# An adaLN attention and mixture-of-experts kernel: sorted tiles transposed by their loads and VectorE, the last three tiles' results brought by products on chip, key and value products four steps later

## The chip, the cores and the metric

The kernel runs on one core of a Trainium2 chip. A core has a TensorE for matrix products, VectorE, ScalarE and GpSimd for the rest, SyncE for issuing transfers, and 16 DMA engines. The metric is the time of one execution on the device in microseconds, as a median over runs. One further execution is taken by the hardware profiler, and the views of the profile and trace come from it.

## What is computed

All data are 32-bit floats. The input is 2 batches of 1024 tokens of 256 numbers. First comes attention, with 16 heads of 128 and one key and value head, on a normalised and modulated input; then a mixture of experts: each token goes to its two best of eight experts.

```python
h = layernorm(x) * (1 + ca) + sa
x = x + ga * attention(h, ...)
h = layernorm(x) * (1 + cb) + sb
logits = h @ router_w.T
topk_vals, topk_idx = top_k(logits, 2); topk_w = softmax(topk_vals)
# rows sorted by expert, then for each expert's rows:
y1 = x_sorted @ w1[e].T                # 256 -> 2 x 176
y2 = (silu(y1[:, :176]) * y1[:, 176:]) @ w2[e].T    # 176 -> 256
y = sum over the two experts of y2 * topk_w
x = x + gb * y
```

## The kernel before

**Attention.** Tokens are cut into 16 tiles of 128. Queries are worked on in four blocks of 512 tokens; in each block a loop runs over 16 heads and 8 key tiles, 128 steps (h, j), each with a product of queries and keys (line 767), an exponential on ScalarE (771) and a product with the values (782). Other work is hung on named steps by `at(h, j, f)`: among it, in the first two blocks, what batch 1's tokens need: normalisation, transposition of the input through DRAM, key and value products (`prep_kv`) and a transposition of the keys (`prep_turned`), at lines 1509 to 1515. In the last block the first twelve token tiles' rows are placed and scattered to DRAM, sorted by expert (`sorted_x`), and the experts' weights are loaded (`load_w1`, line 350). `clear_sorted` (337) fills `sorted_x` with zeros beforehand, in the third block.

**The experts.** The sorted rows make 39 tiles of 128 rows (`ALL`), since each expert's part is rounded up; a row carries 256 numbers and a tail of four: its weight, its place among the results, its batch. Tiles 0 to 16 (`FULL`) hold rows of the first twelve token tiles alone and can be loaded early. Tiles 17 to 38 need the rows of the last four token tiles too, and those are placed and scattered while the first tiles are worked on (`place_second`, eight scatters on GpSimd, hung on the loop at m = 8 and 9). A tile goes through these methods of class `Sorted`:

- `__init__`: one SyncE transfer of 128 rows of 1040 B (1587), issued seven tiles ahead.
- `turn`: two TensorE transposes "xp" (1594) and a ScalarE copy to "xT" (1596), since the product needs the 256 numbers along the partitions.
- `up`: two products "su" of two passes each with the first weight matrix (1603), SiLU on ScalarE "sg" (1611), multiplication on VectorE "sact" (1613).
- `turn_back`: two TensorE transposes "ap" (1619) and a ScalarE copy "sactT" (1621).
- `down`: two products "sy" of two passes each with the second matrix (1628), VectorE's "ysb" (1636), which reads PSUM and multiplies by weight and gate, and an indirect scatter on GpSimd to `results` in DRAM (1639).
- `gates`: VectorE blends the two batches' output gates for tiles 0 to 31 (1656).

The loop at line 1699 emits `turn` of tile m, `up` of m-1, `turn_back` of m-3 and `down` of m-4 (from m = 24 on, one less each). When tile 31's results are scattered, the first twelve token tiles' results can be fetched (`fetch`, 1664, 256 KB a token tile: two rows a token), and `combine` adds the two rows and the residual `xs` on VectorE (1676, 1677) and sends the sum out (1678). The tail (1731 to 1753) adds some of these beside the last tiles, then waits for the last scatter and fetches and adds the last four token tiles.

**What sets the order.** The program names what each engine does, and a planner of the framework puts the instructions of each engine into one order, by modelled costs and the time at which something is due; `tc.issue_after` pins an instruction behind another. Each engine then works through its queue in this order. Transfers from SyncE and ScalarE go over eight lanes in turn, and each waits for the one eight before it. A vector transpose (`turned`, 432, uses it elsewhere) turns each 32 x 32 block of a tile in place of the whole tile.

Of the kernel before, what the change touches and what calls it, by code (L numbers as in the profile page):

```python
# [60 lines left out]
def tile_adaln_attention_moe(  # L61
# [38 lines left out]
    ONES = TOP * SETS[0][1] + E  # L100
    ALL = (TOP * NT * P + E * (P - 1)) // P
    PARTS = 3

    xt = x.rearrange("b (t p) d -> p (b t) d", p=P)
    ot = out.rearrange("b (t p) d -> p (b t) d", p=P)
# [141 lines left out]
    with ExitStack() as attn:  # L247
# [88 lines left out]

        def clear_sorted():

            zero = work.tile([P, ROW], FP, tag="h", name="zero")
            nc.vector.memset(zero, 0.0)  # L340
            by_tile = sorted_x.rearrange("(m p) d -> p m d", p=P)
            nc.sync.dma_start(out=by_tile, in_=zero.unsqueeze(1).to_broadcast([P, ALL, ROW]))
            nobody = work.tile([P, ALL, 1], I32, tag="z", name="nobody")
            nc.gpsimd.iota(nobody, [[P, ALL]], base=TOP * NT * P, channel_multiplier=1)
            with nc.allow_non_contiguous_dma(reason="one number of each row"):
                nc.sync.dma_start(out=by_tile[:, :, TO : TO + 1].bitcast(I32), in_=nobody)
# [1 line left out]
        w1_at = []  # L348

        def load_w1():  # L350
            w1_in = w1.rearrange("(c p) e i -> p c e i", p=P)
            pieces = []
            for c in range(DC):
                piece = keep.tile([P, E, I2], FP, tag="w1" + "ab"[c], name=f"w1_{c}")
                nc.sync.dma_start(out=piece, in_=w1_in[:, c])
                pieces.append(piece)
            w1_at.append(pieces)

# [1075 lines left out]
        for blk in range(NBLK):  # L1434
# [7 lines left out]
            def at(h, j, f, *a):  # L1442
                besides[h * NJ + j].append(lambda: f(*a))
# [62 lines left out]
                    at(QT + 3 + n, 3, on_vector, scatter_some, k, t, 3)  # L1506
                at(HEADS - HG + 1, 0, load_w2)

            for i, h in enumerate(((6, 8, 11, 13), (7, 9, 11, 13))[blk] if blk < 2 else ()):
                t = TPB + blk * QT + i  # L1510
                if t < NT:
                    at(h, 1, prep_norm, t)
                    at(h, 3, prep_input, t)
                    at(h + 1, 5, prep_kv, t)
                    at(h + 1, 7, prep_turned, t)
            last = attention(blk, q, steps, besides)
            settle = Settle(blk)
            if after is None:
# [15 lines left out]
    with ExitStack() as moe:  # L1534
# [28 lines left out]
        def expert(m):  # L1563
# [10 lines left out]
                loaded.update(zip(range(m, m1), values))  # L1574
            return loaded[m]

        class Sorted:


            def __init__(self, m):  # L1580
                self.m = m
                if m < EARLY + NEXT:
                    pool = mx if m < EARLY else me
                    self.x = pool.tile([P, ROW], FP, name=f"x_{m}")
                else:
                    self.x = row_buffer(f"x_{m}")[:, :ROW]
                load = nc.sync.dma_start(out=self.x, in_=sorted_x[ts(m, P), :])
                into_x.read(load, TOP * (SETS[0][1] if m < FULL else NT))

            def turn(self):  # L1590
                m = self.m
                tp = ps_t.tile([P, DC, P], FP, tag="t", name=f"xp_{m}")
                for c in range(DC):
                    nc.tensor.transpose(tp[:, c, :], self.x[:, ts(c, P)], ident)  # L1594
                self.xT = mg.tile([P, DC, P], FP, tag="xT", name=f"xT_{m}")
                nc.scalar.copy(self.xT, tp)  # L1596

            def up(self):
                m = self.m
# [15 lines left out]
            def turn_back(self):  # L1615
                m = self.m
                tp = ps_t.tile([P, 2, P], FP, tag="t", name=f"ap_{m}")
                for c in range(2):
                    nc.tensor.transpose(tp[:, c, :], self.act[:, ts(c, P)], ident)  # L1619
                self.actT = mg.tile([P, 2, P], FP, tag="sactT", name=f"sactT_{m}")  # L1620
                nc.scalar.copy(self.actT, tp)

            def down(self):
                m = self.m
                at = expert(m) * (2 * D)
                y = ps_y.tile([P, D], FP, tag="y", name=f"sy_{m}")
                for c in range(2):
                    nc.tensor.matmul(  # L1628
                        y,
                        self.actT[:, c, :],  # L1630
                        w2_flat[:, c * D :][:, bass.ds(at, D)],
                        start=(c == 0),
                        stop=(c == 1),
                    )
                ysb = mg.tile([P, D], FP, tag="ysb", name=f"ysb_{m}", bufs=5)
                self.evicted = nc.vector.scalar_tensor_tensor(  # L1636
                    ysb, y, self.x[:, WEIGHT : WEIGHT + 1], self.gate, ALU.mult, ALU.mult
                )
                ins = nc.gpsimd.indirect_dma_start(  # L1639
                    out=results,  # L1640
                    out_offset=bass.IndirectOffsetOnAxis(
                        ap=self.x[:, TO : TO + 1].bitcast(I32), axis=0
                    ),
                    in_=ysb,
                    in_offset=None,
                )
                self.scattered = ins.ins
                into_results.add(ins)

            def gates(self):  # L1650

# [9 lines left out]
        def fetch(t, queue=nc.sync):  # L1661

            y = row_buffer(f"y_{t}").rearrange("p (k d) -> p k d", k=TOP)
            load = queue.dma_start(
                out=y,
                in_=results[TOP * t * P : TOP * (t + 1) * P, :].rearrange(
                    "(p k) d -> p k d", k=TOP
                ),
            )
            into_results.read(load, ONES if t < SETS[0][1] else ALL)  # L1670
            return y

        def combine(t, y, queue):

            sum_ = y[:, 0, :]
            nc.vector.tensor_tensor(sum_, sum_, y[:, 1, :], ALU.add)
            nc.vector.tensor_tensor(sum_, sum_, xs[:, t, :], ALU.add)
            queue.dma_start(out=ot[:, t, :], in_=sum_)

        settle.pools(mg, ms, ps_t, "t")  # L1680
        gb_more = mg.tile([P, D], FP, name="gb_more", bufs=1)
        nc.vector.tensor_tensor(gb_more, gb[:, 1, :], gb[:, 0, :], ALU.subtract)
        tiles = []
        fetched, have = [], 0
        back = done = 0
# [9 lines left out]
            7: [lambda: count(NBLK - 1, mg, ps_t, "t"), lambda: place_second(mg, settle.shares)],  # L1695
        }
        SCATTERS = 8
        LATER = 24
        for m in range(ALL + 3):
            there = ALL if m >= SCATTERS + TOP else FULL  # L1700
            while len(tiles) < min(m + 1 + PRE, there):
                tiles.append(Sorted(len(tiles)))
            for f in late.get(m, ()):
                f()
            if m < ALL:
                tiles[m].turn()
            if 0 <= m - 1 < ALL:
                tiles[m - 1].up()
            sooner = m >= LATER
            while back < min(m - 2 + sooner, ALL):  # L1710
                tiles[back].gates()
                tiles[back].turn_back()
                back += 1
            while done < min(m - 3 + sooner, ALL):
                tiles[done].down()
                done += 1
            if SCATTERS <= m < SCATTERS + TOP:
                k = m - SCATTERS
                with tc.issue_after(tiles[done - 1].scattered):
                    if k:  # L1720
                        choose_second(*SETS[1])
                    for t in range(*SETS[1]):
                        scatter(place_i[:, t, k : k + 1], t)

            for t in range(have, min(max(have, 2 * (done - ONES)), SETS[0][1])):
                fetched.append((t, fetch(t)))
                have = t + 1
        assert have == SETS[0][1] and done == ALL


        def added(some, behind, queue):
            with tc.issue_after(behind):
                for t, y in some:
                    combine(t, y, queue)

        BESIDE = 5
        for i in range(BESIDE):
            m = ALL - 4 + i // 2
            added(
                fetched[i : i + 1],  # L1740
                tiles[m].evicted.ins if i % 2 else tiles[m + 1].active.ins,
                nc.sync,
            )
        sent = mg.tile([P, 1], FP, name="sent", bufs=1)
        with tc.issue_after(tiles[-1].scattered):
            nc.gpsimd.memset(sent, 0.0)
        seen = mg.tile([P, 1], FP, name="seen", bufs=1)
        with tc.issue_after(tiles[-1].evicted.ins):
            look = nc.vector.tensor_copy(seen, sent).ins
        lasts = [(t, fetch(t, (nc.sync, nc.scalar)[t % 2])) for t in range(*SETS[1])]  # L1750
        added(fetched[BESIDE:], look, nc.scalar)
        for t, y in lasts:
            combine(t, y, (nc.sync, nc.scalar)[t % 2])


_OUT = ((2, 1024, 256), "float32")
# [41 lines left out]
```

## Time and profile before

| | us |
|---|---|
| median of 3 runs | 1266.76 (1266.58 to 1268.63) |
| the profiled execution | 1273.54 |
| its span | 1271.8 |
| TensorE busy, whole span | 1244.7 (98%) |
| VectorE busy | 848.5 (67%) |
| ScalarE busy | 452.7 (36%) |
| GpSimd busy | 187.3 (15%) |
| expert stage, from about | 1148 |

The span runs from the first to the last record of the profiled execution. Engine names in the profile: PE is TensorE, PEld its weight loads, DVE is VectorE, ACT is ScalarE, POOL is GpSimd, SPq is SyncE's transfer issue. In a row of groups, `out<-in xcount | busy, mean ns | idle before, releaser`, the last field is the idle time of the engine just before these instructions and what ended most of it. In the chain of waits a row is start, length and what ran; in the timeline it is start, length, engine, line, instruction, shape and count, with the idle time before it in brackets. Matmul starts are recorded and their ends modelled, so the pitch of consecutive starts tells more of TensorE's pace than a duration does.

### The profile page before, as it was taken

What the parts mean: (1) busy time and instruction counts of PE and PEld (TensorE: products, weight loads), DVE (VectorE), ACT (ScalarE), POOL (GpSimd) and SP (SyncE); (2) the same over time, 40 slices, a digit from 0 to 9 for tenths busy, and PEclk for the clock granted to TensorE, in tenths of its full rate; (3) what the DMA queues carried; (4) which work ended last, traced back from release to release, by engine and by line L of the source; (5) the groups of instructions that cost most, each with busy time, mean ns of one, the idle gap of its engine ahead of it and who ended that gap; (6) DMA issues with size and microseconds to landing.
All of it is one profiled execution on the core that took longest, in us unless ns stands there. A gap on an engine that the chain in (4) does not pass through costs nothing.

```text
span 1271.8 us, 13505 instructions
## 1 busy us (share of the span) xinstructions
PE 1244.7 (98%) x4134; PEld 686.0 (54%) x4134; DVE 848.5 (67%) x1763; ACT 452.7 (36%) x884; POOL 187.3 (15%) x223
## 2 busy tenths in 40 slices
PE   8999999999999999999999999999999999999895
PEld 5544444448545454548545454557545444477573
DVE  7577777666866876666866666666758675547355
ACT  3533333331333343431333434321333344314331
POOL 3210301010100201010000000000000223204542
PEclk9999999999999999999999999999999999999998
DMA  7011020211011111111011061012011242113426
GB/s 265 0 34 34 6 83 15 73 35 42 13 44 44 40 48 43 49 38 35 12 51 38 34 198 34 34 54 76 13 56 32 68 141 92 34 34 97 134 84 236
DMA packets 87975, 79.26 MB, mean 62 GB/s; under 512 B 43520, under 2 KB 66688, under 8 KB 87648
## 3 DMA queue, kind: packets, MB, share of 16 engines
q1 hardware_dynamic: 82624, 67.06, 17.3%
q0 software_dynamic: 3408, 9.38, 2.0%
q10 hardware_dynamic: 1872, 1.97, 0.4%
q8 instruction: 34, 0.56, 0.2%
q14 instruction: 37, 0.30, 0.1%
HBM read 58.29 MB, written 20.08 MB: 62 GB/s over the span
## 4 chain that ended last, share of the span: by engine, by line
PE 90%; DVE 3%; POOL 2%; issue 2%; DMA 1%; another core or an unknown queue 0%; ACT 0%; SPq 0%; POOLq 0%; DVEq 0%; ACTq 0%
PE s L767 34%; PE o L782 33%; PE q L693 7%; PE pr L925 6%; PE pr L846 2%; PE su L1603 2%; PE sy L1628 1%; POOL results L1639 1%; PE kv L466 1%; PE q L642 1%; PE ap L1619 0%; PE xp L1594 0%; PE lg L1051 0%; DMA wide_q<-row_q 0%; DVE h L404 0%
## 5 line engine op out<-in xcount | busy, mean ns | idle before, releaser
L767 PE MATMUL s<-qT,kT 128*128 128x512 f32 x1024 | 524.4, 595 | 0.7 <-ACT qT L1310 0.7
L782 PE MATMUL o<-p,vs 128*128 128x512 f32 x1024 | 521.6, 592 | 0.0
L771 ACT ACTIVATE p<-s 128x512 f32<-128x512 f32 x512 | 304.8, 597 | 511.3 <-PE s L767 498.1
L787 DVE TENSOR_TENSOR sum<-sum,p 128x512 f32<-128x512 f32 x384 | 264.2, 688 | 178.8 <-ACT p L771 175.9
L782 PEld LDWEIGHTS o<-p,vs 128*128 128x128 f32 x1024 | 194.3, 190 | 243.5 <-issue 238.7
L767 PEld LDWEIGHTS s<-qT,kT 128*128 128x128 f32 x1024 | 191.5, 190 | 186.4 <-issue 177.2
L742 POOL TENSOR_TENSOR rn_q<-rn_q,minus_half 128x16 f32<-128x16 f32 x15 | 44.1, 2940 | 319.0 <-DVE rn_q L738 300.4
L787 DVE TENSOR_TENSOR sum<-p,p 128x512 f32<-128x512 f32 x64 | 43.9, 685 | 38.5 <-ACT p L771 38.5
L1603 PE MATMUL su<-w,xT 128*128 x156 | 54.2, 471 | 3.6 <-ACT xT L1596 3.5
L551 DVE STREAM_TRANSPOSE turned_q<-sq_q 128x512 f32<-128x512 f32 x60 | 42.4, 707 | 18.2 <-ACT sq_q L655 18.2
L925 PE MATMUL pr<-wout_sb,qT 128*128 128x128 f32 x384 | 50.0, 276 | 0.0
L583 DVE TENSOR_TENSOR qT<-qT,wide_q 128x512 f32<-128x512 f32 x60 | 41.1, 686 | 10.7 <-DMA wide_q<-row_q 10.7
L583 DVE TENSOR_TENSOR qT<-qT,wide 128x512 f32<-128x512 f32 x64 | 43.5, 679 | 6.9 <-DMA wide<-row 6.8
L1639 POOL DMA_INDIRECT results<-ysb,x x39 | 40.4, 1037 | 50.5 <-DVE ysb L1636 39.2
L655 ACT ACTIVATE sq_q<-qT 128x512 f32<-128x512 f32 x56 | 35.2, 629 | 34.6 <-DVE qT L700 26.9
L551 DVE STREAM_TRANSPOSE turned<-sum 128x512 f32<-128x512 f32 x64 | 45.5, 710 | 1.8
L925 PEld LDWEIGHTS pr<-wout_sb,qT 128*128 128x128 f32 x384 | 46.2, 192 | 0.1
L693 PE MATMUL q<-rows,wq_sb 128*128 128x256 f32 x168 | 45.4, 379 | 0.0
L789 ACT COPY qT<-o 128x512 f32<-128x512 f32 x64 | 37.4, 584 | 19.7 <-PE o L782 19.6
L552 DVE TENSOR_REDUCE parts<-turned 128x16 f32<-128x512 f32 x64 | 43.3, 676 | 1.1
L1628 PE MATMUL sy<-w2s,sactT 128*128 x156 | 40.3, 383 | 1.5 <-issue 1.3
L552 DVE TENSOR_REDUCE parts_q<-turned_q 128x16 f32<-128x512 f32 x60 | 40.8, 680 | 0.7
(330 smaller groups left out, 1067.9 us busy)
## 6 DMA issues: line engine op xcount, KB each, us to landing
wide<-row SPq DMA_DIRECT2D x64, 256.0 KB
wide_q<-row_q SPq DMA_DIRECT2D x60, 256.0 KB
sorted_x<-zero SPq DMA_DIRECT2D x1, 5070.0 KB
x<-sorted_x SPq DMA_DIRECT2D x39, 130.0 KB
y<-results SPq DMA_DIRECT2D x14, 256.0 KB
w<-in_w_dram SPq DMA_DIRECT2D x2, 1408.0 KB
wout_sb<-in_wout_dram SPq DMA_DIRECT2D x1, 2048.0 KB
wq_sb<-in_wq_dram SPq DMA_DIRECT2D x1, 1536.0 KB
```

The costliest lines, as they stand in the source:

```text
L551: nc.vector.transpose(turned.rearrange("p c k -> p (c k)"), src)
L552: latest["vector"] = nc.vector.tensor_reduce(parts[:, i, :], turned, AX.X, ALU.add).ins
L583: nc.vector.tensor_tensor(q.head(h), q.head(h), wide, ALU.mult)
L693: nc.tensor.matmul(ps[:, k, :].rearrange("p (t k) -> p t k", k=P), x, y, start=True, stop=True,)
L767: latest["tensor"] = nc.tensor.matmul(s, kT[:, ts(b * NJ + j, P)], q.head(h), start=True, stop=True).ins
L771: nc.scalar.activation(p, s, AF.Exp)
L782: latest["tensor"] = nc.tensor.matmul(outs[h], vs[:, b * NJ + j, :], p, start=(j == 0), stop=(j == NJ - 1)).ins
L787: latest["vector"] = nc.vector.tensor_tensor(sums[h], first, p, ALU.add).ins
L925: nc.tensor.matmul(ps[:, piece, :], halves(g)[:, pair, head, t, i, :], w[:, g * HG // TWO + pair, :], start=False, stop=(g == NG - 1 and m ...
L1603: nc.tensor.matmul(u, self.xT[:, c, :], w1_flat[c][:, bass.ds(at, I2)], start=(c == 0), stop=(c == DC - 1),)
L1628: nc.tensor.matmul(y, self.actT[:, c, :], w2_flat[:, c * D :][:, bass.ds(at, D)], start=(c == 0), stop=(c == 1),)
L1639: ins = nc.gpsimd.indirect_dma_start(out=results, out_offset=bass.IndirectOffsetOnAxis(ap=self.x[:, TO : TO + 1].bitcast(I32), axis=0), in ...
```

## The change

- Tiles of sorted rows: for tiles 0 to 7, three transfers each replace one (the tail, and two halves of the 256 numbers written in permuted column order); the TensorE transposes stay. For tiles 8 to 38 five transfers each replace one: the tail of 16 B a row, and four which each fill 32 partitions with 4 x 64 numbers from four rows; then VectorE's transpose of 32 x 32 blocks writes "xT" in one instruction. The rows of the first weight matrix are permuted to match, so that it is loaded by eight transfers in place of two.
- The last three tiles (`HERE`) are no longer scattered. For each, `find` builds a one-hot matrix (128 x 512) of which of the last 512 tokens a row belongs to, and twelve products on TensorE add the three tiles' results into PSUM tiles "direct", which VectorE adds to `xs`. The last four token tiles are therefore fetched after the scatter of tile 35; their rows of `results` are zeroed by `clear_sorted`, since not every row is then written.
- In the first two blocks, `prep_kv` and `prep_turned` are hung four steps later, and the last of the four tiles one head sooner.

```diff
+    HERE = 3
 ...
             nc.sync.dma_start(out=by_tile, in_=zero.unsqueeze(1).to_broadcast([P, ALL, ROW]))
+            lo, hi = [TOP * t * P for t in SETS[1]]
+            nc.sync.dma_start(
+                out=results[lo:hi, :].rearrange("(m p) d -> p m d", p=P),
+                in_=zero[:, :D].unsqueeze(1).to_broadcast([P, (hi - lo) // P, D]),
+            )
...
-            w1_in = w1.rearrange("(c p) e i -> p c e i", p=P)
+            w1_in = w1.rearrange("(b c j) e i -> c b j e i", c=DC, j=SIDE)
...
-                nc.sync.dma_start(out=piece, in_=w1_in[:, c])
+                for b in range(P // SIDE):
+                    nc.sync.dma_start(out=piece[ts(b, SIDE)], in_=w1_in[c, b])
...
-            for i, h in enumerate(((6, 8, 11, 13), (7, 9, 11, 13))[blk] if blk < 2 else ()):
+            for i, h in enumerate(((6, 8, 11, 12), (7, 9, 11, 12))[blk] if blk < 2 else ()):
...
-                    at(h + 1, 5, prep_kv, t)
-                    at(h + 1, 7, prep_turned, t)
+                    at(h + 2, 1, prep_kv, t)
+                    at(h + 2, 3, prep_turned, t)
...
+        FIRST_TILES = 8
+        in_blocks = sorted_x.rearrange("(m a i) d -> m i a d", a=P // SIDE, i=SIDE)
...
-                load = nc.sync.dma_start(out=self.x, in_=sorted_x[ts(m, P), :])
-                into_x.read(load, TOP * (SETS[0][1] if m < FULL else NT))
+                n = D // (P // SIDE)
+                parts = [(self.x[:, D:], sorted_x[ts(m, P), D:])]
+                if m < FIRST_TILES:
+                    src = sorted_x[ts(m, P), :D].rearrange("p (b c j) -> c p b j", c=DC, j=SIDE)
+                    for c in range(DC):
+                        parts.append((self.x[:, ts(c, P)].rearrange("p (b j) -> p b j", j=SIDE), src[c]))
+                else:
+                    for b in range(P // SIDE):
+                        to = self.x[ts(b, SIDE), :D].rearrange("i (a k) -> i a k", k=n)
+                        parts.append((to, in_blocks[m][:, :, ts(b, n)]))
+                for to, src in parts:
+                    with nc.allow_non_contiguous_dma(reason="some numbers of each row"):
+                        load = nc.sync.dma_start(out=to, in_=src)
+                    into_x.read(load, TOP * (SETS[0][1] if m < FULL else NT))
 
             def turn(self):
...
+                nc.vector.transpose(
+                    self.xT.rearrange("p c (a i) -> p a c i", i=SIDE),
+                    self.x[:, :D].rearrange("p (a c j) -> p a c j", c=DC, j=SIDE),
+                )
...
+                if m >= ALL - HERE:
+                    return
                 ins = nc.gpsimd.indirect_dma_start(
...
+            def find(self):
+                half = mg.tile([P, 1], I32, tag="half", name=f"half_{self.m}")
+                nc.vector.tensor_scalar(
+                    half, self.x[:, TO : TO + 1].bitcast(I32), 1, None, ALU.arith_shift_right
+                )
+                token = mg.tile([P, 1], FP, tag="token", name=f"token_{self.m}")
+                nc.vector.tensor_copy(token, half)
+                self.at = mg.tile([P, QB], FP, name=f"at_{self.m}", bufs=1)
+                nc.vector.tensor_scalar(self.at, tokens, token, None, ALU.is_equal)
...
-            into_results.read(load, ONES if t < SETS[0][1] else ALL)
+            into_results.read(load, ONES if t < SETS[0][1] else ALL - HERE)
...
+            if m == TOKENS:
+                nc.gpsimd.iota(token_i, [[1, QB]], base=SETS[1][0] * P, channel_multiplier=0)
+                nc.vector.tensor_copy(tokens, token_i)
+            if FIND <= m - 4 < FIND + HERE:
+                tiles[m - 4 - FIND + ALL - HERE].find()
...
-        lasts = [(t, fetch(t, (nc.sync, nc.scalar)[t % 2])) for t in range(*SETS[1])]
...
+        lasts = [(t, fetch(t)) for t in range(*SETS[1])]
...
+            for tile_ in some:
+                nc.tensor.matmul(
+                    direct[t],
+                    tile_.at[:, ts(i, P)],
+                    tile_.ysb,
+                    start=(tile_ is here[0]),
+                    stop=(tile_ is here[-1]),
+                )
...
+        with tc.issue_after(last_at):
+            for t in range(t0, t1):
+                nc.vector.tensor_tensor(xs[:, t, :], direct[t], xs[:, t, :], ALU.add)
+            for t, y in lasts:
+                combine(t, y, (nc.sync, nc.scalar)[t % 2])
```

More of the change, by code (lines that the diff above doesn't have):

```diff
@@ L102, in tile_adaln_attention_moe @@
     PARTS = 3
+    HERE = 3
+    assert ALL - HERE >= ONES
     xt = x.rearrange("b (t p) d -> p (b t) d", p=P)
@@ L1586, in __init__ @@
                     self.x = row_buffer(f"x_{m}")[:, :ROW]
-                load = nc.sync.dma_start(out=self.x, in_=sorted_x[ts(m, P), :])
-                into_x.read(load, TOP * (SETS[0][1] if m < FULL else NT))
-            def turn(self):
[L1591 to L1596, printed above, removed]
+                n = D // (P // SIDE)
[12 more added lines that the diff above has]
+                    into_x.read(load, TOP * (SETS[0][1] if m < FULL else NT))
+            def turn(self):
+                self.xT = mg.tile([P, DC, P], FP, tag="xT", name=f"xT_{self.m}")
+                if self.m < FIRST_TILES:
+                    tp = ps_t.tile([P, DC, P], FP, tag="t", name=f"xp_{self.m}")
+                    for c in range(DC):
+                        nc.tensor.transpose(tp[:, c, :], self.x[:, ts(c, P)], ident)
+                    nc.scalar.copy(self.xT, tp)
+                    return
[3 more added lines that the diff above has]
+                )
             def up(self):
@@ L1620, in turn_back @@
                 self.actT = mg.tile([P, 2, P], FP, tag="sactT", name=f"sactT_{m}")
-                nc.scalar.copy(self.actT, tp)
+                self.copied = nc.scalar.copy(self.actT, tp).ins
             def down(self):
@@ L1635, in down @@
                 ysb = mg.tile([P, D], FP, tag="ysb", name=f"ysb_{m}", bufs=5)
+                self.ysb = ysb
                 self.evicted = nc.vector.scalar_tensor_tensor(
@@ L1638, in down @@
                 )
+                if m >= ALL - HERE:
+                    return
                 ins = nc.gpsimd.indirect_dma_start(
@@ L1676, in combine @@
             nc.vector.tensor_tensor(sum_, sum_, y[:, 1, :], ALU.add)
-            nc.vector.tensor_tensor(sum_, sum_, xs[:, t, :], ALU.add)
-            queue.dma_start(out=ot[:, t, :], in_=sum_)
+            last = nc.vector.tensor_tensor(sum_, sum_, xs[:, t, :], ALU.add).ins
+            if queue is nc.scalar:
+                with tc.issue_after(tiles[-1].copied):
+                    queue.dma_start(out=ot[:, t, :], in_=sum_)
+            else:
+                queue.dma_start(out=ot[:, t, :], in_=sum_)
+            return last
         settle.pools(mg, ms, ps_t, "t")
@@ L1682, in tile_adaln_attention_moe @@
         nc.vector.tensor_tensor(gb_more, gb[:, 1, :], gb[:, 0, :], ALU.subtract)
+        token_i = mg.tile([P, QB], I32, name="token_i", bufs=1)
+        tokens = mg.tile([P, QB], FP, name="tokens", bufs=1)
         tiles = []
@@ L1697, in tile_adaln_attention_moe @@
         SCATTERS = 8
+        TOKENS, FIND = 20, 27
         LATER = 24
@@ L1728, in tile_adaln_attention_moe @@
         assert have == SETS[0][1] and done == ALL
[L1731 to L1749, printed above, removed]
-        lasts = [(t, fetch(t, (nc.sync, nc.scalar)[t % 2])) for t in range(*SETS[1])]
-        added(fetched[BESIDE:], look, nc.scalar)
-        for t, y in lasts:
-            combine(t, y, (nc.sync, nc.scalar)[t % 2])
+        lasts = [(t, fetch(t)) for t in range(*SETS[1])]
@@ new lines, in tile_adaln_attention_moe, with bring @@
+        direct = {}
+        def bring(t, some):
+            i = t - SETS[1][0]
+            if t not in direct:
+                pool, tag = ((ps_u, "u"), (ps_t, "t"))[i // TWO]
+                direct[t] = pool.tile([P, D], FP, tag=tag, name=f"direct_{t}")
+            for tile_ in some:
[6 more added lines that the diff above has]
+                )
@@ new lines, in tile_adaln_attention_moe @@
+        here = tiles[ALL - HERE :]
+        t0, t1 = SETS[1]
+        for some in (here[:-1], here[-1:]):
+            for t in range(t0, t0 + TWO):
+                bring(t, some)
+        for t in range(t0 + TWO, t1):
+            bring(t, here)
+        behind = [tiles[ALL - 4 + i // 2 + 1 - i % 2] for i in range(5)]
+        behind = [a.evicted.ins if i % 2 else a.active.ins for i, a in enumerate(behind)]
+        behind += [tiles[ALL - 2].evicted.ins]
+        last_at = None
+        for i, (t, y) in enumerate(fetched):
+            with tc.issue_after(behind[i] if i < len(behind) else last_at or tiles[-1].evicted.ins):
+                last_at = combine(t, y, nc.scalar if i >= len(behind) else nc.sync)
```

## The prediction

> **What bounds the kernel now.** I read the engine totals first, then TensorE's costliest groups.
>
> ```profile
> PE 1244.7 (98%) x4134; PEld 686.0 (54%) x4134; DVE 848.5 (67%) x1763; ACT 452.7 (36%) x884; POOL 187.3 (15%) x223
> ...
> L1603 PE MATMUL su<-w,xT 128*128 x156 | 54.2, 471 | 3.6 <-ACT xT L1596 3.5
> ...
> L1628 PE MATMUL sy<-w2s,sactT 128*128 x156 | 40.3, 383 | 1.5 <-issue 1.3
> ```
>
> TensorE is busy for 98% of the span; nothing that only relieves another engine can pay. The expert stage (from 1148 us) is the last tenth of the span. The chain of waits there is TensorE alone:
>
> ```profile
> 1211.42 1.19 PE su L1603 x4
> 1212.61 0.22 PE ap L1619 x2
> 1212.83 0.86 PE sy L1628 x4
> 1213.69 0.22 PE xp L1594 x2
> 1213.91 1.19 PE su L1603 x4
> ```
>
> One tile costs 1.19 + 0.22 + 0.86 + 0.22 = 2.49 us of TensorE with no gap. The reason is the order on its queue: between su_m and ap_m stand the products of other tiles (ap_{m-1}, sy_{m-2}, xp_{m+2} and su_{m+1} in the late part), so SiLU, multiply and copy of tile m run under them. What one tile takes when nothing stands between is read from the timeline, and from the one place where TensorE did wait for the copy:
>
> ```profile
> 1244.69 1.35 PE L1603 MATMUL su<-w,xT 128*128 x4
> ...
> 1246.08 0.32 ACT L1611 ACTIVATE sg<-su 128x176 f32<-128x176 f32 x1 [0.76 <-PE su L1603]
> ...
> 1246.43 0.34 DVE L1613 TENSOR_TENSOR sact<-sg,su 128x176 f32<-128x176 f32 x1 [1.27 <-ACT sg L1611]
> ```
>
> ```profile
> 1180.01 0.37 ACT L1621 COPY sactT<-ap 128x256 f32<-128x256 f32 x1
> ...
> 1180.43 0.92 PE L1628 MATMUL sy<-w2s,sactT 128*128 x3 [0.16 <-ACT sactT L1621]
> ```
>
> After the last pass of su the SiLU starts 1.39 us behind su's start, the multiply 0.35 later; the copy of ap starts 0.47 us behind ap (1245.88 to 1246.35), and sy 0.42 behind that copy.
>
> Last, the waits of TensorE:
>
> ```profile
> PE su L1603 <- ACT xT L1596: 3.5, 2, 2.8
> ...
> PE kv L466 <- DMA rows<-turned_z: 1.2, 1, 1.2
> ```
>
> The 2.8 us belong to a stall over tiles 11 to 15: su_11 to su_15 take 17.63 us instead of 4 x 2.49, so 7.67 too many, with the granted clock at 0.5 for 3.4 us at its end. The profiled execution took 1273.54 us, 6.8 over the median of 1266.76, about this stall. I take it for an event of that execution and work in its times less 7.67 us: su_38 at 1251.94 - 7.67 = 1244.3, end of span 1264.1 = su_38 + 19.86; the median lies 2.7 above.
>
> **The change, part by part.**
>
> *Block loads and vector transposes, the gain intended.* Two TensorE transposes go for 31 tiles: 31 x 0.22 = 6.8 us of the bound engine. The ScalarE copy (0.37) goes, VectorE gets one transpose per tile:
>
> ```profile
> 141.27 0.43 DVE L437 STREAM_TRANSPOSE blocks_z<-z 128x256 f32<-128x256 f32 x1
> ...
> 1148.08 2.22 SPq L1587 DMA_DIRECT2D x<-sorted_x  x5
> ```
>
> VectorE per tile: 0.48 + 0.48 + 0.34 + 0.43 = 1.73 us of 2.49, not a bound by itself. SyncE issues five loads in place of one, 2.22 / 4.67 pitches = 0.475 us each: 2.375 per tile (five of 130 KB in that row go out at this pitch; small ones, the key rows, do as well).
>
> *The order on the queues, where I put the cost.* The instruction order of the changed kernel as built is not the old one less xp. Tiles 8 to 13 keep it; 14 to 16 use up the lead; for tiles 17 to 20 TensorE has su_m, sy_{m-1}, ap_m, su_{m+1}; from tile 21 it has su_m, ap_m, sy_m, su_{m+1}, ap_{m+1}, sy_{m+1}, to the end. On VectorE the transpose of tile m+1 stands behind the multiply of tile m. TensorE takes its queue in order, so nothing covers ScalarE and VectorE any more. One period, from su's start: multiply at 1.39 + 0.35 = 1.74; it takes 0.34 and TensorE follows 0.05 later (the gap in front of the sy row above): ap at 2.13; copy at +0.47 = 2.60; sy at +0.42 = 3.02; sy's passes 0.87: su_{m+1} at **3.9 us**. xT_{m+1} (done 2.08 + 0.43) is ready by then. Against 2.49, each tile loses 1.41, 0.22 saved included. For tiles 17 to 20 the evicting multiply of sy_{m-1} stands before xT_{m+1} on VectorE: su 1.19, sy 0.87 to 2.06, about 0.2 to the eviction, 0.48, gate and transpose 0.43 to 0.9: 3.27 per tile; the step into 21 about 3.46.
>
> *Where the slow part starts.* Tile 17 needs the second set of scattered rows. Copying the token numbers (128x512) adds about 0.55 to VectorE's chain at the stage's start; the transposes of tiles 8 to 10 add 3 x 0.43 = 1.3 in VectorE's solid stretch (1163 to 1175) ahead of the placing; one more result scatter ahead of the set's last four on GpSimd adds its pitch, 1.27. SyncE's first load of x_17, 1186.2 before, is then at some 1188.8; the fifth follows 1.9 later and lands about 2.4 on (single loads took 1.9 to 2.5): 1193.1, plus the transpose and lost lead: su_17 at about 1194.5 (1191.15 before). su_21: 1194.5 + 3 x 3.27 + 3.46 = 1207.8. su_38: 1207.8 + 17 x 3.9 = 1274.1, against 1244.3: **+29.8 us**.
>
> *The last three tiles.* The old end after su_38: the last scatter, 3.59 us to land, and a 2.99 us fetch before the last additions. The new end waits for VectorE: ysb_38 at about su_38 + 5.4, fourteen additions at 0.38 = 5.3, four of the products at 0.42 = 1.7, eight at 0.38 = 3.0, and 3.7 from the last addition to the end as before: 19.1. The twelve products (two passes each, 12 x 0.43 = 5.2 us by a 256-column pass's 0.217) run under these additions but for two that stand ahead of sy_38, 0.9, within the 5.4 counted. Gain 0.8; if VectorE's additions take the 0.42 of single ones, -0.1. The fetches of the last four token tiles start after tile 35's scatter, over 5 us before they are needed at this pace. The finding (three vector operations, at most 0.9 us by a 128x512 row of 0.7) lies in VectorE's slack of 3.9 - 1.73.
>
> *Keys and values four steps later.* They can remove the 1.2 us wait at 165.23, no more: -1.2, between 0 and -1.2. Their products keep their length.
>
> *At nothing:* the eight weight loads in place of two (SyncE has no transfer due there, 352 KB pieces, landed 80 us before use; uncovered they would cost 6 x 0.475), and 1 MB more of cleared rows, about 3 us behind a 15 us write, with SyncE's next transfer 13 us after its end.
>
> *Two rules of the Trainium skill.* First, "DMA: Bandwidth & Descriptors", Rules for kernel authors: coalesce many small transfers, transfers to parts of the partitions use the same engines and gain nothing. The change does the reverse. By the row, issue pitch is 0.475 and the path is not SyncE's while tiles take 3.9: nothing. By the rule (under 64 KB one pays mostly overhead) the five 32 KB pieces would cost up to five of the 1.9 us latencies in sequence, 9.5 per tile; eight are in flight at once, and the key rows of this kernel go out and land eight deep, so I stay with the row. Second, "TensorE: Matmul & The Clock Gate", Why this matters for your kernels: no idle gap over some 3 us, else half clock; its Part 1 adds that frequent short idles between groups can also make the clock swing. Here 2.82 us idle was followed by 0.5, while idle shares of 19 to 24% (1180 to 1184) and of 60 to 65% (1184 to 1188) still showed 1.00. The new gaps are 0.9 and 0.7 us, 42% of each period. By the first rule nothing happens; by the second the passes double: 3.9 + 2.27 = 6.2 per tile, +40 us more. The nearest rows are the gaps of 0.69 and 1.31 us, at full clock; I take no loss and keep the other for the range.
>
> Sum: +29.8 - 0.8 - 1.2 = +27.8; span 1264.1 + 27.8 = 1291.9, plus 2.7: **1294.6 us**.
>
> **Rivals.**
> 1. *It pays (the other side).* If TensorE keeps a lead of one tile, the pace is the larger of 2.27 (no xp) and SyncE's 2.375: 21 x 0.115 us and 9 early tiles x 0.22 are saved, 4.4 us less the late start of about 2, plus 0.8 and 1.2: 1262. The transposes' saving speaks for it, the built order against it. It decides where a tile's period is under 2.49 - 2.6.
> 2. *The order serialises less than worked out*, since part of the waits overlap (instructions on VectorE do by some 0.05 to 0.1 us) or the first tiles go faster: 3.2 to 3.5 per tile, 17 to 21 tiles, 1280 to 1288.
> 3. *The clock falls as well*, in part or all of the 22 tiles: 1303 to 1340.
> 4. *Nothing changes*: loads hidden and order harmless, gains eaten by the late start: 1266.
>
> **How the numbers follow.** The serial pace 0.68 (own range 1288 to 1302, from a period of 3.6 to 4.25 over 22 tiles); rival 2 0.12; rival 3 0.12; rival 1 0.06; rival 4 0.02. The range: 1280 takes in rival 2; up to 1316 a third of rival 3; left out are 0.08 on both rivals below and 0.08 above, 0.16 in all. A measurement of this kernel tells about 0.2% (2.5 us) from no change: faster 0.06, same 0.03, slower 0.91.
>
> **What would show it.** In the timeline of the changed kernel after tile 21: su, ap, sy of one tile in a row; idle of TensorE before ap (by VectorE's sact, about 0.9 us) and before sy (by ScalarE's sactT, about 0.7), 22 times each and more in the list of waits, 30 to 36 us together; TensorE's busy total about 2 us lower; granted clock 1.00 in this stretch; the kv wait gone; su_17 three microseconds later. I would be wrong if those waits are few or short, if TensorE waits for the loads instead (SyncE's queue or the vector transpose named), or if the clock falls to a half there.

## The result

| | us |
|---|---|
| before, median of 4 runs | 1266.74 (1266.58 to 1268.63) |
| changed kernel, median of 4 runs | 1301.49 (1299.60 to 1302.48) |
| ratio, 95% interval | 1.0270 (1.0257 to 1.0283) |
| changed kernel, profiled execution and its span | 1302.01, 1300.1 |

The change costs 34.7 us, 2.7%. 1294.6 was predicted, +27.8, with a range from 1280 to 1316.

The first lines of the page of the changed kernel, engine totals and the groups that answer to those shown of before:

```profile
PE 1254.1 (96%) x4096; PEld 683.4 (53%) x4096; DVE 860.8 (66%) x1807; ACT 441.7 (34%) x853; POOL 183.0 (14%) x220
...
L1638 PE MATMUL su<-w,xT 128*128 x156 | 55.0, 476 | 4.7 <-DVE xT L1628 3.0
...
L1663 PE MATMUL sy<-w2s,sactT 128*128 x156 | 42.7, 394 | 9.3 <-ACT sactT L1656 9.3
```

The idle time before sy was 1.5 us and is 9.3. The waits of TensorE from tile 21 to 38 alone (1211 to 1283 us) show where it stands:

```profile
PE ap L1654 <- DVE sact L1648: 12.8, 17, 0.8
PE sy L1663 <- ACT sactT L1656: 8.8, 17, 0.5
PE su L1638 <- PE sy L1663: 1.0, 3, 0.3
```

Columns: total, how often, the longest. Neither wait was in the list of before at more than 0.5 us. Now they come once a tile. The chain of waits of the changed kernel over one tile, which before was TensorE alone, now goes round four engines' instructions:

```profile
1249.52 1.20 PE su L1638 x4
...
1250.74 0.33 ACT sg L1646
...
1251.09 0.35 DVE sact L1648
...
1251.49 0.45 PE ap L1654 x2
...
1252.02 0.38 ACT sactT L1656
...
1252.44 1.13 PE sy L1663 x4
1253.57 1.20 PE su L1638 x4
```

From one su to the next are 4.05 us, with every engine waiting for another. Starts of su's first pass in the trace give the whole stretch: su_17 at 1197.34, su_21 at 1211.69, su_38 at 1282.39, so 70.7 us for 17 tiles, 4.16 each; most take 4.05, and every fourth 4.5.

The clock had no part in that. The table of stretches of the changed kernel has, between the time slices and TensorE's busy time and count, its granted clock (the last columns are DMA share and GB/s):

```profile
1212.00:1232.00 20.00, 13.63 (x50) 1.00 0.44 92
1232.00:1252.00 20.00, 13.60 (x50) 1.00 0.28 63
1252.00:1282.00 30.00, 20.17 (x73) 1.00 0.46 160
```

TensorE idles for 32% of the time and keeps the full clock.

### The profile page after: what moved, and what is told of

It reads as the page before. It is cut to its first block, busy times and chain, and to the rows that moved or that the text cites. A ratio compares the mean times of both kernels' runs of the same rounds, so it can differ in the third digit from the quotient of the medians.

```text
span 1300.1 us, 13555 instructions
## 1 busy us (share of the span) xinstructions
PE 1254.1 (96%) x4096; PEld 683.4 (53%) x4096; DVE 860.8 (66%) x1807; ACT 441.7 (34%) x853; POOL 183.0 (14%) x220
## 2 busy tenths in 40 slices
DMA packets 115271, 79.92 MB, mean 61 GB/s; under 512 B 74880, under 2 KB 94080, under 8 KB 114944
## 4 chain that ended last, share of the span: by engine, by line
PE 90%; DVE 4%; SPq 1%; ACT 1%; issue 1%; POOL 1%; DMA 1%; DVEq 0%; ACTq 0%; POOLq 0%
PE s L779 33%; PE o L794 33%; PE q L705 7%; PE pr L937 6%; PE su L1638 2%; PE sy L1663 2%; PE pr L858 2%; SPq L1617 1%; PE ap L1654 1%; PE kv L478 1%; ACT sactT L1656 1%; PE q L654 1%; DVE sact L1648 0%; ACT sg L1646 0%; DVE y L1726 0%
## 5 line engine op out<-in xcount | busy, mean ns | idle before, releaser
L1677 POOL DMA_INDIRECT results<-ysb,x x36 | 35.4, 984 | 72.6 <-DVE ysb L1672 46.7
```

## The experiments

Each was run beside the kernel before on the same chip, and its ratio is to those runs. Chips differ: the kernel before had a median of 1274.59 us on the chip of the two runs that change TensorE's order alone, of its own second profile and of the run with TensorE's transposes kept; 1266.98 on that of the run with fewer loads and of the direct products alone; 1267.51 on that of the rest.

**The order of TensorE alone, in the kernel before.** Loads, transposes and tail are untouched; for tiles 25 to 38 one tile's su, ap and sy are put in a row (with xp of the next tile between ap and sy). `downed` is the last product sy of a tile.

```diff
+            if m > LATER:
+                sooner = 2
+                if m - 1 < ALL:
+                    with tc.issue_after(tiles[done - 1].downed):
+                        tiles[m - 1].up()
...
-            while done < min(m - 3 + sooner, ALL):
+            while done < min(m - 3 + sooner + (sooner == 2), ALL):
```

> The kernel before with nothing changed but TensorE's order for tiles 25 to 38: su_m, ap_m, sy_m of one tile in a row (xp of the next one between ap and sy). Theory (order alone): a tile takes 4.0 us there, as in the changed kernel, in place of 2.49, 14 tiles: +21 to +24 us, 1288 to 1291. Rival (loads or vector transposes are what costs): no change, 1267.

Measured: 1296.80 us, ratio 1.0168 (1.0149 to 1.0186), +22.2 us; 4.05 us a tile, with every fourth at 4.4. One tile in this trace:

```profile
1233.04 0.32 ACT L1611 ACTIVATE sg<-su 128x176 f32<-128x176 f32 x1 [2.13 <-PE su L1603]
1233.39 0.34 DVE L1613 TENSOR_TENSOR sact<-sg,su 128x176 f32<-128x176 f32 x1 [0.53 <-ACT sg L1611]
...
1233.78 0.44 PE L1619 MATMUL ap<-ident,sact 128*128 128x128 f32 x2 [0.78 <-DVE sact L1613]
...
1234.73 1.13 PE L1628 MATMUL sy<-w2s,sactT 128*128 x4 [0.30 <-ACT sactT L1621]
```

The same 0.78 us before ap as in the changed kernel. So the order is enough to bring this pace, without block loads and without VectorE's transposes; the loss is within the 21 to 24 us expected of it.

**The order of TensorE put back, in the changed kernel.** First as in the prediction: only the order on TensorE, and the transpose xT of tile m ahead of the multiply of m-1. `turned` is a tile's xT, `upped` its last su, `backed` its last ap.

```diff
+                    with tc.issue_after(tiles[m].turned):
                         tiles[m - 1].up()
...
+                with tc.issue_after(tiles[min(m - 1, ALL - 1)].upped):
                     tiles[back].turn_back()
...
+                with tc.issue_after(tiles[back - 1].backed):
                     tiles[done].down()
```

> The changed kernel with its loads, vector transposes, direct products and kv steps, but with TensorE's order pinned as in the kernel before (su_m, ap_m-2, sy_m-3, from the late tiles su_m, ap_m-1, sy_m-2) and xT_m pinned ahead of sact_m-1 on VectorE. Theory (the lost lead costs the time): a tile takes 2.27 to 2.5 us again, the stretch from su_17 to su_38 falls from 85 us to about 50, the time is 1264 to 1270. Rival (five loads a tile, SyncE's queue or landing): a tile keeps over 3 us, TensorE waits for xT, 1283 and above.

Measured: 1298.89, ratio 1.0191 (1.0174 to 1.0208), so +24.3 us on its chip. The changed kernel was not run there; elsewhere it is 34.7 and 37.0 above the kernel before, so TensorE's order alone took back about a third. A tile took mostly 3.5 to 4.1 us, 3.74 on average from su_21 to su_38: the rival's number, though not its reason. Two lines of the timeline of this kernel and the one after them on TensorE:

```profile
1252.73 0.48 DVE L1672 SCALAR_TENSOR_TENSOR ysb<-sy,x,gate 128x256 f32<-128x256 f32 x1 [2.47 <-PE sy L1663]
...
1253.65 0.44 DVE L1628 STREAM_TRANSPOSE xT<-x 128x256 f32<-128x256 f32 x1
...
1254.23 1.42 PE L1638 MATMUL su<-w,xT 128*128 x4 [1.54 <-DVE xT L1628]
```

The transpose itself waited for nothing: it stood on VectorE behind the eviction ysb of two tiles back, and that had waited 2.47 us for the sy which TensorE works on just before this su. Most of the loss had only moved to the other queue: sy, then ysb, then xT, then su.

So the transpose was emitted one tile sooner and pinned ahead of that eviction as well:

```diff
-                tiles[m].turn()
+                tiles[m + 1].turn()
...
+                    with tc.issue_after(tiles[m + 1].turned):
                         tiles[done].down()
```

> As e1_lead, and the vector transpose now emitted two tiles ahead (xT_m+1 in the step of su_m-1) and pinned ahead of sact_m-1 and of the eviction of the sy in that step, so that on VectorE no xT stands behind an eviction that waits for the sy just before its su. TensorE's order is the one before. Theory (the lead is lost in two queues, TensorE's and VectorE's, and nothing else costs): 2.3 to 2.6 us a tile from 21 to 38, 26 us less than the changed kernel, within 5 us of the kernel before. Rival (SyncE's five loads or their landing are the bound once the order is right): over 2.8 us a tile, TensorE or VectorE waiting for x.

> The changed kernel as it is, for its ratio to the kernel before on the same chip as the runs beside it. Expected: 25 to 35 us slower than the kernel before, with 4.05 us a tile from tile 21 and every fourth tile some 0.45 longer.

Measured, on one chip: the changed kernel 1304.52, ratio 1.0297 (1.0281 to 1.0313); with both orders put back 1269.63, ratio 1.0020 (1.0011 to 1.0029). The changed kernel is 37.0 above the kernel before, 2 more than the upper end expected, and 34.9 of them are gone, with every load and every vector transpose still there. Tiles 7 to 15 took 2.27 us each, and so did most after tile 18. In this timeline of one tile, xT of a later tile is made under su, and ap and sy follow su without a gap:

```profile
1200.12 1.35 PE L1638 MATMUL su<-w,xT 128*128 x4
1200.46 0.45 DVE L1628 STREAM_TRANSPOSE xT<-x 128x256 f32<-128x256 f32 x1 [0.88 <-DMA x<-sorted_x]
...
1201.30 0.38 PE L1654 MATMUL ap<-ident,sact 128*128 128x128 f32 x2
...
1201.52 1.03 PE L1663 MATMUL sy<-w2s,sactT 128*128 x4
...
1202.39 1.35 PE L1638 MATMUL su<-w,xT 128*128 x4
```

What remains is a new bound. VectorE's waits from 1190 to 1250 and SyncE's issues in this kernel:

```profile
DVE xT L1628 <- DMA x<-sorted_x: 23.2, 18, 5.6
```

```profile
1186.88 55.99 SPq L1617 DMA_DIRECT2D x<-sorted_x  x110
1243.23 12.45 SPq L1714 DMA_DIRECT2D y<-results  x16
```

SyncE issued the 110 loads of 22 tiles in 55.99 us with hardly a pause. Starts are mostly 0.475 us apart and five times 0.63 to 1.85, so 0.509 us each on average, 2.545 a tile, more than the 2.49 of the kernel before. From su_17 to su_38 this kernel took 53.49 us for 21 tiles, 2.547 each, the pace of that queue. And the fetches of the results, queued behind them, began only at 1243.2, less than a tile ahead of su_38 (1245.05).

**Fewer loads on that queue.** The four numbers behind each row are loaded for four tiles at once (tiles 17 to 38), 94 transfers in place of 110.

```diff
+                    if g == 0:
+                        rows_ = sorted_x[m * P : (m + n_) * P, D:]
+                        parts.append((tails[:, :n_, :], rows_.rearrange("(g p) d -> p g d", p=P)))
+                    self.tail = tails_at[-1][:, g, :]
```

> e5_lead3 with the four-number tails of tiles 17 to 38 loaded four tiles at a time, so that SyncE issues 4.25 loads a tile in place of five. In e5_lead3 SyncE issued 110 loads in 55.99 us without a pause, 0.509 us each, 2.545 a tile. Theory (with the order right SyncE's issue is the bound): 94 loads take 48 us, a tile 2.27 to 2.35 us from 18 on, su_38 some 3 us sooner than in e5_lead3, the fetches of the results some 8 us sooner, the time 4 to 6 us less than e5_lead3's, 2 to 4 us below the kernel before. Rival (the landing of small pieces or VectorE is the bound, not the issue): no change against e5_lead3, within 1.5 us.

Measured: 1265.78, ratio 0.9990 (0.9980 to 0.9999): 1.2 us below the kernel before, at the edge of what can be told. Against the kernel with five loads, by the two ratios and so across chips, it is 3.8 us less. Both are a little short of what was expected, 2 to 4 and 4 to 6. Tiles after 18 took 2.27 us nearly throughout, and xT's waits for loads fell:

```profile
DVE xT L1642 <- DMA x<-sorted_x: 6.1, 3, 5.6
```

The number of issues was the bound: what is moved is the same (115015 packets in the execution against 115271), and only the issues are fewer. What is left of the transposes' 6.8 us is little, for two reasons in this trace: su_17 still has to wait for the second set of rows (its first pass starts 4.26 us after the last one of su_16, at 1191.57, where 1.38 us is usual), so what tiles 8 to 16 save is given back there; and the fetches start at 1237.4, so that VectorE's additions fall behind the last tile (21.2 us from su_38 to the end, where the changed kernel takes 17.75).

**The ring of evicted results.** As the kernel with both orders put back, with `bufs=8` for ysb in place of 5.

> e5_lead3 with eight buffers in place of five for the evicted results (ysb), so that an eviction waits for the scatter of eight tiles before. Theory (the stall at tiles 12 to 16 is the eviction waiting for a results scatter that stands behind the second set's scatters on GpSimd): su_11 to su_17 is shorter by 3 to 6 us than in e5_lead3. Rival (signals between engines are late in that stretch for another reason): no change, within 1.5 us.

Measured: 1269.92, ratio 1.0015 (1.0006 to 1.0025), as without it; su_11 to su_17 took 17.5 us against 16.5. The ring does not set the time in this stretch there. That kernel has no stall at tiles 11 to 15, so this does not tell what the ring does in the changed kernel.

**The kernel before, profiled again.**

> The kernel before once more, for a second profile. If the 7.7 us stall at tiles 11 to 15 belongs to the first profiled execution alone, the span is about 1265 us and su_11 to su_15 take close to 4 x 2.49 = 10 us. If it belongs to the program (VectorE's eviction waiting for a results scatter that stands behind the second set's scatters on GpSimd), they take again 12 us and more, and the same wait is seen.

Measured: span 1269.8 in 1272.24 us, beside medians of 1274.59; su_11 to su_15 took 16.2 us, so the stall at tiles 11 to 15 was there again. In the trace of the next kernel, which is the kernel before in everything but the kv steps and ran on another chip, the same four tiles took 9.96 us, without it. All four profiles from the chip with the median of 1274.59 have the stall (16.2 to 20.1 us for these four tiles, whatever the kernel), and none of the six from the two other chips of the experiments (at most 10.9). On the chip of the result it was in one profiled execution 6.8 us above the median. So it goes with a chip or an execution, and not with one of these edits; what brings it stays open.

The kv kernel loses time a little later instead: from su_15 to su_17 it took 8.92 us, where 4.98 is usual. TensorE's transposes of tile 17 waited for that tile's load, and the granted clock was 0.50 from 1192 to 1194:

```profile
1190.03 0.41 PE L1594 MATMUL xp<-ident,x 128*128 128x128 f32 x2 [1.59 <-DMA x<-sorted_x]
```

**The key and value steps alone, and the direct products alone,** each in the kernel before.

> The kernel before with the key and value products and the key transpositions four steps later and nothing else. Theory: the 1.2 us wait of TensorE for kv's rows is gone and the time falls by 0.5 to 1.2 us, at most 0.1%. Rival: no difference that can be told, because what is saved there comes back as another wait.

> The kernel before with the direct products of the last three tiles alone (find, the one-hot products, the zeroed rows of results, the tail's new order); single loads, TensorE's transposes and the kv steps as before. Theory (the prediction's sum): su_38 to the end takes 17.0 to 17.9 us in place of 19.3 to 19.9, so 1.5 to 2.5 us gained, less up to 0.6 for the copied token numbers: 0.1% faster. Rival (it costs as much in VectorE as it saves in the end): no difference that can be told.

Measured: the kv steps 1267.35, ratio 1.0000 (0.9991 to 1.0009). The wait is gone and others have come; TensorE's waits in this kernel over the attention blocks:

```profile
PE sums_q L560 <- DVE parts_q L552: 0.9, 3, 0.6
```

In place of the 1.2 us before kv, at 165 us, there are 0.9 us before the sums of the queries' squares, the longest at 213, which the list of before does not have. The first su starts 0.2 us sooner than in the first trace of the kernel before. That is the rival.

The direct products: 1265.94, ratio 0.9991 (0.9982 to 1.0000), 1.0 us less, at the edge of what can be told. From su_38 to the end are 17.75 us (1245.87 to 1263.62), as the theory had it.

**Both together with TensorE's transposes kept** (three loads a tile, `FIRST_TILES = ALL`; the planner then keeps the old order):

> The changed kernel with the three permuted loads and the TensorE transposes kept for all 39 tiles; the direct products of the last three tiles and the kv steps stay. As built, TensorE's order is then the old one with its lead. Theory: 2.49 us a tile, and the gains of the other two parts remain (1.2 for the kv wait, about 2 for the end): 1263 to 1266. Rival (the direct products, the find or the kv steps cost part of the 35 us): above 1270.

Measured: 1276.02, ratio 1.0012 (1.0002 to 1.0021), 1.4 us slower than the kernel before on its chip. This is neither what was expected nor the rival's value. The end was 17.05 us after su_38, but su_11 to su_17 took 25.1 us in its profile against 21.1 in the kernel before profiled beside it: the stall, larger, as in every profile from this chip. A further 1.45 us went between su_17 and su_38, at tiles 24 to 26. Whether the three loads bring these or the chance of these executions was not separated.

## Why the prediction was right, step by step

The sum was worked in a frame of the kernel before without its stall, su_17 at 1191.15 and su_38 at 1244.3. The trace of the kv kernel, which is the kernel before from tile 0 on and has no stall at tiles 11 to 15, puts them at 1194.92 and 1248.04 with the end at 1267.32. Against this trace the changed kernel, profiled in the same set of runs (su_17 1197.02, su_21 1211.36, su_38 1282.03, end 1299.76), gives:

| step | predicted | measured |
|---|---|---|
| su_17 later | +3.4 | +2.1 |
| tiles 17 to 20 | +3.3 | +4.4 (14.34 for 9.96) |
| tiles 21 to 37 | +23.1 | +27.5 (70.67 for 43.16) |
| su_38 to the end | -0.8 | -1.6 (17.73 for 19.28) |
| kv wait (by the run of the kv steps alone) | -1.2 | 0 |
| sum | +27.8 | +32.4 (medians there +37.0) |

The profiled execution of the changed kernel was the fastest of its runs and that of the kv kernel the slowest of its own, which is the difference to the medians.

*su_17.* The 2.1 hang on the trace that is taken: the kv kernel loses 3.9 us of its own at tiles 15 and 16. In the trace of the direct products alone, which loses 0.7 there, su_17 starts at 1192.30, 4.7 us before that of the changed kernel. The prediction's reason was not the one that acted. It had the first load of x_17 go out at 1188.8 (its parts, 0.55, 1.3 and 1.27 behind 1186.2, make 1189.3); in the first trace of the changed kernel it went out at 1186.69. In the kernel with both orders put back it went out at 1186.88, and su_17 started at 1191.56. In the changed kernel something else held su_17 back, the stall told of below, so that the nearness of the number is luck.

*Tiles 17 to 20.* 3.24 to 3.34 us a tile against 3.27. The 1.1 us missing are in the step into tile 21: 4.47 where the prediction put 3.46 without a working. TensorE reads expert numbers there.

*The order on the queues.* Right, and shown from both sides: it brings 4.05 us a tile to the kernel before, and putting it back on both queues takes 34.9 of 37.0 us away. The term was mis-sized. 3.9 us were predicted, and it is 4.05 with 4.5 at every fourth tile, 4.16 on average. The parts, from the chain above: su to sg 1.22, to the multiply 0.35, to ap 0.40, to the copy 0.53 (0.47 predicted), to sy 0.42, and to the next su 1.13 in the chain's cut, which is 0.97 by the start of that su's first pass (0.87 predicted). After an idle gap the second pass comes 0.1 us late: the sy passes start at 1252.44, 1252.76, 1252.98 and 1253.19, so 0.32 and then 0.22 apart. The first weight load, elsewhere done under the pass before, stands in the open here (`LDWEIGHTS` and pass both start at 1252.44), which fits, but was not tried. The every-fourth tile is where TensorE reads the expert numbers of the next four tiles; the kernel with the serial order alone has it as well, and before it lay under other work. Over the 17 tiles three of these take 4.53 to 4.56 and five others 4.12, so 17 x 0.15, 3 x 0.49 and 5 x 0.07, the 4.4 us missing.

*The signs it named.* The two waits came where it said, once a tile, but at 0.78 and 0.52 us in place of 0.9 and 0.7, and at 21.6 us together over 17 tiles in place of 30 to 36 over 22. TensorE's busy total did not fall by 2 us: it rose by 9.4, from 1244.7 to 1254.1. A tile takes 4.05 us, its products alone 2.27 (the pace with both orders put back), and of the 1.78 between them only 1.30 are recorded as idle. The rest stands in the modelled durations: in the chain ap takes 0.45 for 0.22 before, and sy 1.13 for 0.86.

*What it took to undo it* was not seen in the prediction. It named TensorE's queue as the place, and xT as ready by then; the run with only that order put back is still 24.3 us above the kernel before, so that VectorE's order has to be put right as well for most of the gain.

*Five loads at 0.475.* In the row of 110 the usual pitch was 0.475 as read; the five longer ones, whose cause stays open, make 0.509 on average, 2.545 a tile: hidden at 4.05 as the prediction had it, but the rival that needs a pace of 2.375 would not have reached it. It would have been a bound at about the old pace, as the run with both orders showed. The rule of the Trainium skill that the prediction weighed ("DMA: Bandwidth & Descriptors", Rules for kernel authors: under 64 KB one pays mostly overhead) thus had a point that the single row of five did not show: what counted was the issue, not five latencies in sequence, which the prediction put at 9.5 us a tile. Nor are there five pieces of 32 KB a tile, as it says, but four and a tail of 2 KB.

*The end.* The gain was 1.6 us against this trace, and 1.2 and 2.1 against the two profiles of the kernel before, where 0.8 was predicted; alone in the kernel before it makes 1.0 us.

*Keys and values.* Wrong: the wait was removed, and 0.9 us of waiting came up before other products. The prediction had put its gain at the upper end of a bound that it had named itself, 0 to 1.2.

*The clock.* Right: gaps of 0.78 and 0.52 us, a third of the time, left it at 1.00, and the 6.2 us a tile that the prediction worked out for a halved clock did not come.

*At nothing.* The eight weight loads and the cleared rows were not tried alone. The kernel with both orders put back has them, and is 2.1 us above the kernel before in all.

*The stall as an event of one execution.* Only partly right: it is in two profiles of the kernel before out of two, though its second profile was taken on a chip that shows it in every kernel. The changed kernel has a stall of its own a little later, where su_15 to su_17 take 11.33 us. In that one the trace names a cause:

```profile
1189.81 0.48 DVE L1672 SCALAR_TENSOR_TENSOR ysb<-sy,x,gate 128x256 f32<-128x256 f32 x1 [3.86 <-DMA results<-ysb,x]
```

An eviction waits for a results scatter, which on GpSimd had stood behind the second set's scatters; behind it on VectorE stands xT_16. The prediction had not named that wait. That it holds up su_17 is read from the trace; no run took it away in this kernel. su_16 then ran at the lower clock that is told of at the end.

## What to carry to other kernels

Before adding the cost of single operations, read the order in which each engine takes its queue in the program as built: a software pipeline that holds an engine at 98% is a property of that order, and a planner can drop it when one operation moves to another engine or one load becomes five. Look for the lead in every in-order queue of the loop, since here it had to be put back on TensorE and on VectorE: TensorE's alone left 24.3 us of the loss, both left 2.1. And count a queue's issues per unit of work: 110 loads of 0.509 us on average became the bound as soon as the other was gone.

## What the runs showed of the hardware

Signals between engines came late in one stretch. In the run with TensorE's order alone put back, su_11's last pass started at 1176.35, and its SiLU only at 1179.83; the transposes of ap_9 started at 1176.65 and 1176.76, and ScalarE's copy of them only at 1182.77, with nothing but that one SiLU on ScalarE in between. Elsewhere in that trace SiLU follows the last pass by about 0.5 us, and the copy follows its transposes by about 0.4. It was the time in which GpSimd issued scatters nearly back to back (nine between 1176.4 and 1186.9). The stalls at tiles 11 to 15 in the kernel before have such delays too, between TensorE's transposes and ScalarE's copy of them. Scatters at this pitch are not enough to bring them: in the trace of the kv kernel there are twelve between 1176.8 and 1191.4, and SiLU follows the last pass by 0.50 us at every tile from 11 to 15. The delays are in the first profile of the kernel before and in the four from the chip where it takes 1274.59 us, and in none of the other seven. Their cause stays open.

After a longer gap the clock fell. In the changed kernel TensorE was busy for 1.42 of the 4 us from 1188 to 1192, with a wait of 2.57 us for sact; from 1192 to 1196 the granted clock was 0.57 and 0.58.
